# A masked-attention layer on one core: one sum behind the masks, first loads, bias and normalising moved, a decode and residual additions at the end by GpSimd

## The chip, the cores and the metric

The kernel runs on one core of a Trainium2 chip. The metric is device time in microseconds, as the median of several runs. The engines are TensorE (PE in the profile, with its weight loads as PEld), VectorE (DVE), ScalarE (ACT), GpSimd (POOL) and SyncE (SP), whose queue issues nearly all transfers. Each works through its own list in order; they wait for each other by semaphores.

## The reference

```python
# x, adj: (128, 128, 768) and (128, 128, 128); Wq, Wk, Wv: 768 x 768; H = 12 heads of HD = 64
h = jnp.maximum(_layernorm(x, axis=-1), 0.0)
q, k, v = (_split_heads(h @ W + b) for W, b in ((Wq, bq), (Wk, bk), (Wv, bv)))
scores = jnp.einsum('bhqd,bhkd->bhqk', q, k) / jnp.sqrt(HD)
scores = scores + beta * adj[:, None]
scores = jnp.where(adj[:, None] > 0, scores, -9000000000000000.0)
probs = jax.nn.softmax(scores, axis=-1)
out = jnp.einsum('bhqk,bhkd->bhqd', probs, v)
return x + out.transpose(0, 2, 1, 3).reshape(x.shape)
```

All of it is float32.

## The kernel before

**Groups and slices.** The 128 graphs are worked through in 32 groups of four (`GRP`, index `G`). Each group has three slices: `qk0` makes the queries and keys of heads 0 to 5, `v` the values of all heads, `qk1` the queries and keys of heads 6 to 11. The attention of a group is woven into the slices that follow its products.

**Products.** A slice is a product of the group's normalised activations with weights. The first group does it plainly (`plain_slice`, L845), and DVE and POOL meanwhile make sums of weight blocks, which are written to DRAM (`kept`). From the second group on (`product_z`, L550) each slice is 15 products with fewer multiplications than the plain way: product `n` of the list `PRODUCTS` takes one sum of activation blocks (`S0`, `S7`, ... or a block itself, `A00`, ...) and one prepared sum of weights (`T7`, `B01`, ..., read back from DRAM through a ring of five buffers by `load_T`, L338, or resident). The four chains "a" to "d" accumulate in a PSUM pair each, out of four pairs; scores and attention take their pairs from the same four, in the order in which pairs are given back.

**Evacuation.** After each product its result is taken to the output chunks that it belongs to, named (r, j). The first product of a chunk copies it, on ACT (L568 and two L570 with the bias); each later one adds to it on DVE (L574). Product 10 (S0) adds to chunk (0, 2), product 6 (A00) subtracts from it, product 7 (S7) adds to (0, 0). When a chunk has its last product, it is decoded in four additions (`decode`, L592 to L595), on POOL or, for some products, on DVE.

**What stands where.** The order of products in a slice is a list: `PORDER` for `qk0` and `v`, `ZORDER` for the second group's `qk0`, `QORDER` for `qk1`, `LORDER` for the last group's `qk1`. All other work is hung by hand on the positions of these lists: `then(at, ...)` puts it between the product's matmuls and its evacuation, `then((at, "post"), ...)` behind the evacuation. In each position the order of emission is: matmuls, masks that are due, work hung there, decodes and additions that are due, evacuation, exponentials that are due, the work hung behind. Thus the order on each engine is fixed. The work around the change is

- `sum_acts` (L467, DVE): an activation sum; S7 = A01 - S10 and S0 = S1 - S6 of the group,
- `scores` (L629, PE) and behind it the mask (L637, DVE), which reads the scores' PSUM pair, adds the bias of the adjacency and gives the pair back; the exponential (L639) follows on ACT,
- `attend` (L686, PE), which takes a pair at the next product and is woven into its matmuls; L695, L697 and L669 on ACT sum, copy and divide, `add` (L711, DVE) adds the residual, `send` stores,
- `norm` (L449, ACT): the normalisation and relu of the next group, in eight pieces of 192 columns for two graphs; `to_hT` (L462, DVE) transposes them,
- `halve_bias` (L977, POOL): a difference of the value bias, needed by the first `product_z` slice `v`.

In `qk0` of the third and later groups, scores stand at position 2 (twice) and behind position 6; S7 is hung at position 0, S0 at position 1.

**The end.** The last group's `qk1` is followed by attention in halves: `scores_half` (L738), its mask (L743) and `attend_half` (L759 on PE, L656 and L657 on DVE, `o_last` L669 on ACT, the addition L789 on DVE).

Of the kernel before, what the change touches and what calls it, by code (L numbers as in the profile page):

```python
# [14 lines left out]
ALU = mybir.AluOpType  # L15
# [4 lines left out]
GRP = 4  # L20
# [91 lines left out]
PORDER = (1, 0, 5, 2, 3, 10, 7, 6, 13, 11, 4, 9, 14, 8, 12)  # L112
ORDER = {"qk0": PORDER, "v": PORDER, "qk1": QORDER}
RING = 5
# [12 lines left out]
def direct(ctx, tc, x, adj, wq, bq, wk, bk, wv, bv, beta, out, bad):  # L127
# [10 lines left out]
    nc = tc.nc  # L138
    B, N, D = x.shape
    HD = D // HEADS  # L140
# [128 lines left out]
    def prepare(sl):  # L269
# [47 lines left out]
        for first, then_finish in PREPARED:  # L317
            for name in first:
                steps.append(lambda name=name: sums(name))
            for name in then_finish:  # L320
                steps.append(lambda name=name: finish(name))
# [123 lines left out]
    def norm(G, g, lo=0, hi=NB):  # L445
        for b in range(lo, hi):
            t = xg[G, g][:, b, :]
            n = g * NB + b
            nc.scalar.activation(t, t, AF.Relu, bias=shift[G, n], scale=rstd[G, n])  # L449

    def home_A(G, name):
        if (G, name) in wide:
            return A[G, name]
        t = wide[G, name] = work.tile([P, 2 * GRP, P], F32, tag=name, name=f"{name}_{G}", bufs=1 + (name[1] == "0"))
        full[G, name] = t[:, 0:7]
        A[G, name] = t[:, GRP:2 * GRP].rearrange("p (c g) n -> p c (g n)", c=2)
        return A[G, name]
# [76 lines left out]
    def product_z(G, sl, n):  # L534
# [21 lines left out]
        for (r, j), sign in uses:  # L556
# [19 lines left out]
            if not left[key]:  # L576
                last = order_of(G, sl) is LORDER
                engine = nc.vector if sl == "qk1" and (n == 12 or last and n in (11, 13, 14)) else nc.gpsimd
                later(lambda r=r, j=j, engine=engine: decode(G, sl, r, j, engine), 1 if last else LAG.get((sl, n), 1))
# [96 lines left out]
    def attend_steps(G, oc, behind):  # L676
# [14 lines left out]
        o = e.rearrange("p i w -> p (i w)")[:, 0:8 * VE].rearrange("p (r b e) -> p r b e", r=2, e=VE)  # L691
        t = xo[G, oc]

        def leave_pair():
# [15 lines left out]
        def add():  # L710
            nc.vector.tensor_tensor(t, t.rearrange("p g (i d) -> p g i d", i=2),  # L711
                                    o[:, :, :, 0:HD].rearrange("p r (g i) d -> p (r g) i d", i=2), ALU.add)

        def send():
            nc.sync.dma_start(out[G * GRP:(G + 1) * GRP, :, oc * P:(oc + 1) * P].rearrange("g n d -> n g d"), t)

        ends = G == NG - 1
        later(add, behind)
# [28 lines left out]
    def attend_half(G, oc, r, late, now=True):  # L747
# [30 lines left out]
        def sum_up():  # L778
# [9 lines left out]
            else:  # L788
                nc.vector.tensor_add(t, t, o.rearrange("p (b j) d -> p b (j d)", j=2))  # L789
            send()  # L790
# [160 lines left out]
    def half(step):  # L951

        if step == 0:
            for g in range(2, GRP):
                stats(0, g)
        elif step == 1:
            first["got"] = moments_1(0, 2 * NB, 4 * NB)
        else:
            first["pool"] = moments_2(0, 2 * NB, 4 * NB, *first["got"])
            for g in range(2, GRP):  # L960
                norm(0, g)
            for k in range(3):
                first["dve"] = to_hT(0, 1, k)
# [20 lines left out]
    def then(at, f, *args):  # L984
        todo.setdefault(at, []).append(lambda: f(*args))
# [72 lines left out]
    for n in range(18):  # L1058
        then(n, step, 2 - (n > 8))
    then(1, halve_bias)  # L1060
    sums_at(1, ((12, "S1"), (13, "S9"), (14, "S10"), (15, "S2")))
# [4 lines left out]
    bias(1, 4, 6, 8)  # L1066
    for n in range(RING):
        then(10 + n, load_T)
    plain_slice(0, "qk1", todo, (1, 0))

    for G in range(1, NG):
# [5 lines left out]
        attention(G - 1, 1, ((7, 2), (10, 0), (12, 1)))  # L1077
        sums_at(G, ((0, "S7"), (1, "S0"), (5, "S5"), (8, "S14"), (9, "S11")))
        if G == 1:
            todo[0].insert(0, lambda: sum_acts(1, "S6"))  # L1080
        if more:
            for n, at in enumerate((1, 2, 4, 5)):
# [198 lines left out]
```

## Time and profile before

| | us |
|---|---|
| median of 3 runs | 2697.48 |
| the runs | 2691.35, 2700.34, 2697.48 |
| the profiled execution | 2692.31 |
| its span, first to last instruction | 2690.5 |
| PE busy | 2650.9 |
| DVE busy | 2185.2 |
| POOL busy | 2111.8 |
| ACT busy | 1751.2 |

The profile is of one execution. A matmul's end is modelled, so that a busy PE is not yet a PE at its peak; a wait shows where an engine had nothing to do until another released it. Line numbers are those of the kernel before.

### The profile page before, as it was taken

Reading aid. Unit: us, or ns where it says so; the run is one execution under the profiler, and the core shown is the slowest. Engines: PE = TensorE matmul, PEld = TensorE weight load, DVE = VectorE, ACT = ScalarE, POOL = GpSimd, SP = SyncE. Lnnn points to the kernel's source line nnn. Section 1 sums busy time; section 2 is a strip of 40 time slices with the busy share of each in tenths; the row PEclk is TensorE's granted clock in tenths of the full one; section 3 lists DMA queues with packets and bytes.
Section 4 is the critical chain, followed back from the end, with each engine's and each line's share of the span. In section 5 each row is a group of like instructions: output and inputs, shape, how many; then the busy total and the mean of one; then the engine's idle time right before and its main releaser. Section 6 shows DMA issues by size and latency. Waiting matters only on the chain.

```text
span 2690.5 us, 121410 instructions
## 1 busy us (share of the span) xinstructions
PE 2650.9 (99%) x52029; PEld 2564.3 (95%) x52029; DVE 2185.2 (81%) x2705; ACT 1751.2 (65%) x4612; POOL 2111.8 (78%) x3034
## 2 busy tenths in 40 slices
PE   8999999999999999999999999999999999999997
PEld 7799999999999999999999999999999999999997
DVE  6878888878888788888788877788887888887886
ACT  2576766677666677666766666776667676667553
POOL 4867878877888778788778787787887787887783
PEclk9999999999999999999999999999999999999999
DMA  9889888989889898889898888888898988898875
GB/s 228 275 258 280 276 273 271 275 277 272 270 268 286 262 285 274 272 275 281 264 279 279 264 272 271 271 279 271 278 273 267 278 283 270 272 284 268 257 238 155
DMA packets 530341, 721.71 MB, mean 268 GB/s; under 512 B 105980, under 2 KB 374024, under 8 KB 529800
## 3 DMA queue, kind: packets, MB, share of 16 engines
q1 hardware_dynamic: 528640, 713.12, 85.9%
q8 instruction: 411, 6.73, 1.0%
q10 hardware_dynamic: 1160, 0.79, 0.2%
q14 instruction: 130, 1.06, 0.1%
HBM read 647.73 MB, written 66.05 MB: 265 GB/s over the span
## 4 chain that ended last, share of the span: by engine, by line
PE 77%; DVE 13%; DMA 3%; issue 2%; POOL 1%; ACT 0%; SPq 0%; POOLq 0%; DVEq 0%; ACTq 0%
PE pair L550 67%; PE pair L686 5%; PE pair L629 5%; DVE home L574 4%; DVE sbig L467 3%; DVE e L637 1%; DMA T_qk<-kept_qk 1%; DMA T_v<-kept_v 1%; DMA out_dram<-xo 1%; DVE xo L711 1%; DVE home L595 1%; DVE home L593 1%; DVE home L592 1%; DVE sbig L574 0%; DVE home L594 0%
## 5 line engine op out<-in xcount | busy, mean ns | idle before, releaser
L574 DVE TENSOR_TENSOR home<-home,pair 128x896 f32<-128x896 f32 x810 | 860.9, 1076 | 276.0 <-PE pair L550 236.9
L550 PE MATMUL pair<-sbig,T_qk 128*64 128x128 f32 x13020 | 827.8, 273 | 9.7 <-DVE e L637 7.3
L550 PEld LDWEIGHTS pair<-sbig,T_qk 128*64 128x64 f32 x13020 | 708.0, 137 | 20.9 <-DVE e L637 14.0
L550 PE MATMUL pair<-A,T_qk 128*64 128x128 f32 x6944 | 463.7, 273 | 0.0
L669 ACT ACTIVATE e<-e,sm 128x64 f32<-128x64 f32 x1512 | 382.0, 343 | 111.7 <-DVE sm L657 111.5
L592 POOL TENSOR_TENSOR home<-home 128x256 f32<-128x256 f32 x297 | 265.8, 895 | 226.2 <-DVE home L574 222.2
L550 PE MATMUL pair<-T_v,sbig 128*64 128x128 f32 x6944 | 418.3, 274 | 5.5 <-issue 2.8
L686 PE MATMUL pair<-v,e 128*64 128x65 f32 x6048 | 401.8, 221 | 0.5 <-DVE e L637 0.5
L550 PEld LDWEIGHTS pair<-T_v,sbig 128*64 128x64 f32 x6944 | 381.5, 137 | 20.1 <-issue 17.4
L568 ACT ACTIVATE home<-pair 128x640 f32<-128x640 f32 x325 | 231.2, 711 | 260.3 <-PE pair L550 200.0
L550 PEld LDWEIGHTS pair<-A,T_qk 128*64 128x64 f32 x6944 | 378.1, 137 | 5.9 <-issue 5.5
L686 PEld LDWEIGHTS pair<-v,e 128*64 128x64 f32 x6048 | 359.8, 137 | 3.9 <-DVE e L637 1.0
L550 PE MATMUL pair<-sbig,res_qk 128*64 128x128 f32 x4340 | 288.5, 273 | 0.0
L593 POOL TENSOR_TENSOR home<-home 128x256 f32<-128x256 f32 x297 | 248.4, 836 | 23.3
L595 POOL TENSOR_TENSOR home<-home 128x256 f32<-128x256 f32 x297 | 240.3, 809 | 23.3
L550 PEld LDWEIGHTS pair<-sbig,res_qk 128*64 128x64 f32 x4340 | 234.6, 137 | 5.3 <-issue 5.3
L695 ACT ACTIVATE sm<-pair,tiny 128x8 f32<-128x8 f32 x189 | 49.3, 261 | 286.9 <-PE pair L686 286.9
L594 POOL TENSOR_TENSOR home<-home 128x128 f32<-128x128 f32 x297 | 213.9, 720 | 23.3
L449 ACT ACTIVATE x<-x,block 128x192 f32<-128x192 f32 x480 | 231.8, 553 | 0.0
L637 DVE SCALAR_TENSOR_TENSOR e<-pair,biasT 128x1024 f32<-128x1024 f32 x189 | 225.0, 1216 | 3.2 <-PE pair L629 3.2
L639 ACT ACTIVATE e<-e 128x1024 f32<-128x1024 f32 x189 | 193.7, 1065 | 47.0 <-DVE e L637 39.1
L472 POOL TENSOR_TENSOR A<-A 128x256 f32<-128x256 f32 x186 | 169.9, 914 | 59.2 <-DVE A L462 59.2
(197 smaller groups left out, 4604.3 us busy)
## 6 DMA issues: line engine op xcount, KB each, us to landing
T_qk<-kept_qk SPq DMA_DIRECT2D x713, 448.0 KB, 4.9
T_v<-kept_v SPq DMA_DIRECT2D x341, 448.0 KB, 4.7
xo<-in_x_dram SPq DMA_DIRECT2D x189, 256.0 KB, 4.4
out_dram<-xo SPq DMA_DIRECT2D x189, 256.0 KB, 6.0
x<-in_x_dram SPq DMA_DIRECT2D x248, 192.0 KB, 6.7
sbig<-in_x_dram SPq DMA_DIRECT2D x116, 384.0 KB, 6.3
kept_qk<-prep_qk SPq DMA_DIRECT2D x23, 448.0 KB, 2.9
adj<-in_adj_dram SPq DMA_DIRECT2D x128, 64.0 KB, 4.5
```

The source lines that it names most:

```text
L449: nc.scalar.activation(t, t, AF.Relu, bias=shift[G, n], scale=rstd[G, n])
L550: nc.tensor.matmul(p[q:q + HD, at, :], lhs[:, q:q + HD], rhs, start=(first and at % 4 == 0), stop=True, skip_group_check=True)
L568: nc.scalar.activation(t[:, 0:5], p[:, 0:5], AF.Copy, scale=float(sign))
L574: nc.vector.tensor_tensor(t, t, p[:, 0:7], op)
L592: e.tensor_tensor(t[:, 1:4:2], t[:, 1:4:2], twice(5), ALU.add)
L593: e.tensor_tensor(t[:, 2:5:2], t[:, 2:5:2], twice(1), ALU.add)
L594: e.tensor_tensor(t[:, 4], t[:, 4], t[:, 6], ALU.add)
L595: e.tensor_tensor(t[:, 0:7:6], t[:, 0:7:6], twice(2), ALU.add)
L637: nc.vector.scalar_tensor_tensor(e, ps, SCORE_CAP * ISCALE, bias, op0=ALU.min, op1=ALU.add)
L639: trailing.append(lambda: nc.scalar.activation(e, e, AF.Exp, scale=1.0 / ISCALE))
L669: nc.scalar.activation(o[:, r, b, 0:HD], pa[:, r, b, 0:HD], AF.Copy, scale=t[:, 1, r, b:b + 1])
L686: nc.tensor.matmul(pa[q:q + HD, 2 * g + i, :], k[:, q:q + HD], vt[G, "v", r, h // 4][:, 4 * g + h % 4, :], start=True, stop=True, skip_gro ...
```

## The change

- Third to last group, `qk0`: products 7 and 6 change places (`XORDER`); S0 is hung at position 0 and S7 behind position 4. In the second group the sums move likewise, its order stays.
- First group: of the third and fourth graph's normalisation DVE does the third's (four scale-and-shift pieces and one maximum), ACT the fourth's. The first two loads of prepared weights are issued between two steps of the preparation instead of at positions 10 and 11 of the first `qk1`. The steps behind them come up to two places later. The bias step moves to position 4 of the second group's `qk0`.
- Last group: the decode behind product 13 and the residual additions of three chunks and of two halves go from DVE to POOL.

```diff
 PORDER = (1, 0, 5, 2, 3, 10, 7, 6, 13, 11, 4, 9, 14, 8, 12)
-ORDER = {"qk0": PORDER, "v": PORDER, "qk1": QORDER}
+XORDER = (1, 0, 5, 2, 3, 10, 6, 7, 13, 11, 4, 9, 14, 8, 12)
+ORDER = {"qk0": XORDER, "v": PORDER, "qk1": QORDER}
...
             for name in first:
                 steps.append(lambda name=name: sums(name))
+            if sl == "qk1" and first[0] == "T0":
+                steps += [load_T, load_T]
...
+    def norm_dve(G, g):
+        for b in range(NB):
+            t = xg[G, g][:, b, :]
+            n = g * NB + b
+            nc.vector.tensor_scalar(t, t, rstd[G, n], shift[G, n], op0=ALU.mult, op1=ALU.add)
+        t = xg[G, g]
+        nc.vector.tensor_scalar(t, t, 0.0, None, op0=ALU.max)
...
-                engine = nc.vector if sl == "qk1" and (n == 12 or last and n in (11, 13, 14)) else nc.gpsimd
+                engine = nc.vector if sl == "qk1" and (n == 12 or last and n in (11, 14)) else nc.gpsimd
...
         def add():
-            nc.vector.tensor_tensor(t, t.rearrange("p g (i d) -> p g i d", i=2),
-                                    o[:, :, :, 0:HD].rearrange("p r (g i) d -> p (r g) i d", i=2), ALU.add)
+            e = nc.gpsimd if ends and oc < 3 else nc.vector
+            t2 = t.rearrange("p g (i d) -> p g i d", i=2)
+            e.tensor_tensor(t2, t2, o[:, :, :, 0:HD].rearrange("p r (g i) d -> p (r g) i d", i=2), ALU.add)
...
-                nc.vector.tensor_add(t, t, o.rearrange("p (b j) d -> p b (j d)", j=2))
+                (nc.gpsimd if now else nc.vector).tensor_tensor(t, t, o.rearrange("p (b j) d -> p b (j d)", j=2), ALU.add)
...
-            for g in range(2, GRP):
-                norm(0, g)
+            norm_dve(0, 2)
+            norm(0, 3)
...
-    then(1, halve_bias)
...
-    for n in range(RING):
+    for n in range(2, RING):
         then(10 + n, load_T)
...
-        sums_at(G, ((0, "S7"), (1, "S0"), (5, "S5"), (8, "S14"), (9, "S11")))
+        sums_at(G, ((0, "S0"), ((4, "post"), "S7"), (5, "S5"), (8, "S14"), (9, "S11")))
         if G == 1:
             todo[0].insert(0, lambda: sum_acts(1, "S6"))
+            then(4, halve_bias)
```

More of the change, by code (lines that the diff above doesn't have):

```diff
@@ L692, in attend_steps @@
         t = xo[G, oc]
+        ends = G == NG - 1
         def leave_pair():
@@ L710, in add @@
         def add():
-            nc.vector.tensor_tensor(t, t.rearrange("p g (i d) -> p g i d", i=2),
-                                    o[:, :, :, 0:HD].rearrange("p r (g i) d -> p (r g) i d", i=2), ALU.add)
+            e = nc.gpsimd if ends and oc < 3 else nc.vector
+            t2 = t.rearrange("p g (i d) -> p g i d", i=2)
+            e.tensor_tensor(t2, t2, o[:, :, :, 0:HD].rearrange("p r (g i) d -> p (r g) i d", i=2), ALU.add)
         def send():
             nc.sync.dma_start(out[G * GRP:(G + 1) * GRP, :, oc * P:(oc + 1) * P].rearrange("g n d -> n g d"), t)
-        ends = G == NG - 1
         later(add, behind)
```

## The prediction

> **What bounds the kernel now.** I read the busy times first, then the stretches, then who waited for whom, then one group on three engines.
>
> ```profile
> span 2690.5 us, 121410 instructions
> ...
> PE 2650.9 (99%) x52029; PEld 2564.3 (95%) x52029; DVE 2185.2 (81%) x2705; ACT 1751.2 (65%) x4612; POOL 2111.8 (78%) x3034
> ```
>
> ```profile
> 0.00:207.00 207.00, 196.49 (x2431) 168.84 (x2433) 157.67 (x288) 99.03 (x250) 139.50 (x232) 0.99 0.87 253
> ```
>
> ```profile
> 288.60:370.10 81.50, 81.20 (x1650) 79.45 (x1648) 67.37 (x80) 55.47 (x146) 66.05 (x95) 1.00 0.89 276
> ```
>
> ```profile
> 2591.00:2690.50 99.50, 85.03 (x1688) 79.94 (x1684) 66.40 (x116) 44.34 (x124) 42.98 (x66) 0.94 0.59 180
> ```
>
> In the last three rows the first number after the stretch is its length, the second the time in which TensorE (PE) was busy. PE is busy for 2650.9 of 2690.5 us, so all that a rearrangement can win is the remaining 39.6 us. Of these, 10.5 us lie in the first 207 us (the first two groups), 14.5 us in the last 99.5 us, and in the middle a group of 81.5 us has 0.3 us of idle PE. The change removes no matmul; it can only move these waits. Which of them it can move, the waits of the weight loads say best, since they run ahead of the matmuls and show the whole gap:
>
> ```profile
> PEld pair L550 <- DVE e L637: 14.7, 29, 0.7
> ```
>
> So 29 times PE waits for a mask (L637), 14.7 us in all, 0.51 us each: once in each group from the fourth on. This is what "a sum behind the masks" aims at. Here is the place in one group, PE first, then VectorE (DVE), ScalarE (ACT) and GpSimd (POOL); columns are start, duration, engine, line, what is written from what, count, and the idle time before with its releaser.
>
> ```profile
> 298.09 1.98 PE L629 MATMUL pair<-home 64*64 64x128 f32 x64
> ...
> 302.05 4.81 PE L550 MATMUL pair<-sbig,T_qk 128*64 128x128 f32 x84 [0.30 <-DVE e L637]
> 306.79 1.10 PE L629 MATMUL pair<-home 64*64 64x128 f32 x32
> 307.82 1.75 PE L550 MATMUL pair<-A,T_qk 128*64 128x128 f32 x28
> ...
> 309.62 0.40 PE L686 MATMUL pair<-v,e 128*64 128x65 f32 x8
> ```
>
> ```profile
> 298.17 1.42 DVE L467 TENSOR_TENSOR sbig<-A,sbig 128x896 f32<-128x896 f32 x1
> 299.52 1.34 DVE L467 TENSOR_TENSOR sbig<-sbig 128x896 f32<-128x896 f32 x1
> 300.79 2.34 DVE L637 SCALAR_TENSOR_TENSOR e<-pair,biasT 128x1024 f32<-128x1024 f32 x2
> ...
> 303.95 1.07 DVE L574 TENSOR_TENSOR sbig<-sbig,pair 128x896 f32<-128x896 f32 x1
> 304.95 1.08 DVE L467 TENSOR_TENSOR sbig<-A,sbig 128x896 f32<-128x896 f32 x1
> 307.00 1.09 DVE L574 TENSOR_TENSOR home<-home,pair 128x896 f32<-128x896 f32 x1 [0.97 <-PE pair L550]
> 308.01 1.22 DVE L637 SCALAR_TENSOR_TENSOR e<-pair,biasT 128x1024 f32<-128x1024 f32 x1
> ```
>
> ```profile
> 302.06 0.72 ACT L568 ACTIVATE home<-pair 128x640 f32<-128x640 f32 x1
> ...
> 303.15 2.04 ACT L639 ACTIVATE e<-e 128x1024 f32<-128x1024 f32 x2
> 305.04 1.02 ACT L449 ACTIVATE x<-x,block 128x192 f32<-128x192 f32 x2
> 305.92 0.74 ACT L568 ACTIVATE home<-pair 128x640 f32<-128x640 f32 x1
> 306.50 0.67 ACT L570 ACTIVATE home<-pair,bqk 128x128 f32<-128x128 f32 x2
> ```
>
> The two sums S7 (298.17) and S0 (299.52) stand ahead of the two masks on DVE. The first mask ends at 300.79 + 2.34/2 = 301.96, and the product at position 4 (the x84 row, three products), which takes the PSUM pair that this mask gives back, starts at 302.05.
>
> **Steady groups: the wait goes, and another one takes most of its place.** With S7 gone from there, S0 starts at 298.2 and the first mask about 1.3 us earlier, well before the pair is wanted. PE starts positions 4 to 6 0.51 us sooner. S7 itself (1.08 by the row at 304.95, which has no other work beside it) fits between the evacuation at 303.95 and the next sum: both sums are done by about 306.5, and product 7, now at position 7, wants S7 only at 307.3. So far the gain is the whole 0.51 us.
>
> But the new order also puts product 6 (A00) at position 6, right behind product 10 (S0) at position 5. Both write the same chunk, (0, 2): product 10 comes first, so ACT evacuates it (305.92 and 306.50, two L570 ending at 307.17), and product 6 is then added to it by DVE. In the old order product 7 stood between, whose evacuation adds to another chunk and waited for PE alone (the row at 307.00). The new evacuation must wait for ACT. ACT is not moved by the change: from the row at 302.06 on it works without a gap, on things queued before the masks matter. So the evacuation begins at about 307.21, 0.21 later than now, and the third mask, queued behind it on DVE, ends at 308.01 + 1.22 + 0.21 = 309.44 instead of 309.23. The attention at 309.62 takes the pair that this mask gives back. PE, 0.51 us early, would want it at 309.11; it gets it at about 309.49 (a mask's end to PE took 0.09 in the x84 row, less with the pair of masks rounded: I take 0.05). What remains of 0.51 is 0.13 us. For the 28 groups before the last of these that is 3.6 us; the last group has no normalisation of a following one on ACT (L449), so there the whole 0.5 us stays. The third group does not wait for a mask now, and may get the new wait: 0.3 us back. Sum: 3.8 us. Ends: 0 (ACT 0.13 us later than I think) and 14.7 us (ACT not in the way). S0 a slot earlier, and (0, 2) decoded a slot earlier by POOL, cost nothing: POOL sits idle before that decode,
>
> ```profile
> 310.86 1.51 POOL L592 TENSOR_TENSOR home<-home 128x256 f32<-128x256 f32 x1 [6.23 <-DVE home L574]
> ```
>
> for 6.23 us. If that cover were gone, the chunk is needed only in the next slice.
>
> **First group and the way into the second.**
>
> ```profile
> 28.43 3.61 ACT L449 ACTIVATE x<-x,shift,rstd 128x192 f32<-128x192 f32 x8 [3.12 <-POOL shift L397]
> ```
>
> ```profile
> 32.08 1.90 DVE L462 STREAM_TRANSPOSE A<-x 128x512 f32<-128x512 f32 x3 [5.71 <-ACT x L449]
> ...
> 112.30 0.68 DVE L493 TENSOR_SCALAR adj<-biasT 128x512 f32<-128x512 f32 x1
> ```
>
> ```profile
> 32.84 15.81 PE L845 MATMUL pair<-A,sbig 128*128 128x256 f32 x72 [1.53 <-DVE A L462]
> ...
> 115.75 0.45 PE L686 MATMUL pair<-v,e 128*64 128x65 f32 x8 [0.51 <-DVE e L637]
> ...
> 126.93 1.75 PE L550 MATMUL pair<-sbig,T_qk 128*64 128x128 f32 x28 [0.89 <-DMA T_qk<-kept_qk]
> 128.89 4.80 PE L550 MATMUL pair<-sbig,T_qk 128*64 128x128 f32 x84 [0.20 <-DMA T_qk<-kept_qk]
> ...
> 136.24 1.70 PE L550 MATMUL pair<-sbig,T_qk 128*64 128x128 f32 x28
> ```
>
> ACT's eight normalisations take 3.61 us; half of them 1.8. DVE, idle for 5.71 us, does the other half beside it: by the 0.68 us for 512 columns, four of 192 columns about 0.25 each and one maximum over 768 about 1.0, together 2.0 us or less. The transposes start 1.6 us earlier, and PE's 1.53 us go. The two early loads of weights go out where SP's queue stands still for the prepared sums; they wait only for buffers whose writes are queued ahead of them, and take away 0.89 + 0.20 us. What stands behind them on SP, a residual load and later prepared writes, waits for GpSimd or is needed much later. Without the bias step (below) GpSimd, and through its prepared sums DVE, run about 1.4 us ahead there, so that the 0.51 us at 115.75 go too. That makes 3.1 us.
>
> ```profile
> 96.45 1.45 POOL L977 TENSOR_TENSOR bv_b<-bv_b 128x384 f32<-128x384 f32 x1
> ```
>
> The bias step lands in the second group at position 4, where POOL is idle; its first user is the V slice. But in the second group product 7 stays at position 5 (its order is not changed), and S7 is now queued after position 4, behind a mask:
>
> ```profile
> 135.79 1.21 DVE L637 SCALAR_TENSOR_TENSOR e<-pair,biasT 128x1024 f32<-128x1024 f32 x1
> ```
>
> The mask can start only when the scores before position 4 are done; mask and sum, 1.2 + 1.05, run against one product of 1.6 us (three took 4.74 us from 302.05 to 306.79). So PE waits there at least 0.7 us, and about 1.5 if DVE is a microsecond behind as it is now. Sum for this part: 3.1 - 1.5 = 1.6 us gained, between -0.5 and 2.8.
>
> **The end.**
>
> ```profile
> 2661.60 0.72 POOL L595 TENSOR_TENSOR home<-home 128x256 f32<-128x256 f32 x1
> ```
>
> ```profile
> 2662.20 0.67 PE L738 MATMUL pair<-home 64*64 64x128 f32 x16
> ```
>
> ```profile
> 2663.93 0.42 DVE L592 TENSOR_TENSOR home<-home 128x256 f32<-128x256 f32 x1
> ...
> 2665.16 0.42 DVE L595 TENSOR_TENSOR home<-home 128x256 f32<-128x256 f32 x1
> ...
> 2668.53 0.43 DVE L789 TENSOR_TENSOR xo<-xo,o_last 128x256 f32<-128x256 f32 x1 [1.06 <-ACT o_last L669]
> ...
> 2673.47 0.42 DVE L789 TENSOR_TENSOR xo<-xo,o_last 128x256 f32<-128x256 f32 x1 [1.05 <-ACT o_last L669]
> ```
>
> From 2662 on DVE sets the pace. It loses a decode (2663.93 to 2665.58, 1.6 us), an addition behind it, and the two halves' additions with the waits for ACT before them, 1.49 and 1.47 us. Not all of it is on the path: with the decode gone DVE waits for PE's product instead, and of the two waits the second counts. On the other side GpSimd now does a 128x512 addition (about 1.4 us, twice the 0.72 for 256 columns) ahead of the decode that ends at 2662.3 and that the scores at 2662.20 wait for: PE and all after it get 1.3 us later there. Followed through, the third half's scores come 0.25 us earlier, the fourth's 0.75, the last two 2.1 us earlier, and the tail with them. I take 2.0 us, between 0 and 2.5.
>
> A rule of the Trainium skill speaks against this part: "SBUF — State Buffer", section "Who interferes with whom", says that a DVE instruction with two SBUF inputs and a GpSimd instruction that reads SBUF exclude each other, the second waiting until the first has ended. The trace agrees so far: the same 128x256 operation of GpSimd took 1.51 us at 310.86, beside DVE's sums, and 0.72 at 2661.60. By that rule each GpSimd addition at the end could hold up a DVE decode for its whole length; only one, of 256 columns, meets a decode in the order that I followed, so by the rule the end would gain 1.3 and the sum be 6.7 instead of 7.4.
>
> **Sum.** 3.8 + 1.6 + 2.0 = 7.4 us. The profiled execution took 2692.31 us, 5.2 less than the median 2697.48 of the three runs; it becomes 2684.9, and the median 2690.1. A measurement of this kernel tells about 0.3%, 8.1 us, from no change, so the likeliest case stands just on that border.
>
> **Rivals.** (a) The masks' wait goes and nothing follows: if ACT's evacuation of product 10 ends before PE has done product 6, the groups keep 14.7 us. For it speaks that 0.4 us less on ACT would do; against it that ACT has no gap there. 14.7 + 1.6 + 2.0 = 18.3 us, median 2679.2. (b) Slower: the evacuation that now waits for ACT ends later still. The point from which it decides is 0.13 us beyond the 307.21 at which I let it begin. ACT has a pair of normalisations of 1.02 us right ahead (305.04); if one more piece of 0.6 us comes between on ACT, each group is 0.47 us longer than now, 28 groups 13.2 us, less the 3.6 at both ends: 9.6 us slower, 2707.1 at the median. Against it: no ACT instruction in the groups is added or moved. (c) The part in the groups does nothing at all and start and end cancel (POOL's delay before the scores, S7 in the second group): 2697.
>
> **How the numbers follow.** My case 0.58, (a) 0.2, (b) 0.12, (c) 0.1. My case spreads by some 3 us, so about half of it, 0.3, is beyond 0.3% faster, and a little of it, 0.01, slower. With (a) this makes 0.5 for faster. (b) gives 0.1 to slower; with 0.03 for what I have not seen, 0.14. The rest is 0.36. The range goes from 2677, just past (a), to 2698, past (c); it leaves out (b) and what lies beyond (a).
>
> **What would show it.** Right: in the waits, the 14.7 us of L550 for the mask shrink below 2, and a new entry of about 0.4 us, some 28 times, appears for the attention's matmuls behind a mask; on DVE the evacuation at position 6 names ACT as its releaser; a group is 0.1 us shorter. At the start the 1.53 us of idle PE are gone; in the second group position 5 waits for a sum; at the end the scores wait 1.1 us or more for a GpSimd decode and DVE's two additions with their waits for ACT (1.06 and 1.05) are gone. Wrong: groups 0.5 us shorter with no new wait (a), or longer (b).

## The result: 0.3% faster, as forecast, but not by the terms of its sum

| | us |
|---|---|
| before, median of 6 runs | 2695.86 (2691.35 to 2700.34) |
| after, median of 6 runs | 2685.23 (2683.14 to 2687.57) |
| after / before | 0.9968, 95% interval 0.9957 to 0.9978 |
| profiled execution before and after | 2692.31, 2685.37 |
| its span before and after | 2690.5, 2683.5 |

The forecast was 2690.1, between 2677 and 2698. The medians of the table differ by 10.6 us, but before's lies high in its six runs: in the 23 runs that it had beside four of the experiments its median was 2692.01, and 2685.23 is 6.8 us or 0.25% below that. The two profiled executions differ by 6.9 us where the sum said 7.4, so that the gain lies on the border of 0.3%, as forecast. That agreement is luck in part: of the three terms the one on which most of the argument was spent is nearly gone, and the other two are larger.

Most line numbers of after are 11 to 12 higher: L561 is the product (L550), L640 the scores (L629), L697 the attention (L686), L648 the mask (L637), L478 the sums (L467), L585 the adding evacuation (L574), L579 and L581 ScalarE's (L568, L570), L452 the normalisation (L449, only 3 higher), L458 and L460 VectorE's share of it (new), L750 the halves' scores (L738), L603 to L606 the decode, L725 and L801 the additions (L711, L789), L709 ScalarE's copy of an attention pair (L697). In the kernel without the early loads they are 2 lower than in after.

The page after the change, and the three stretches that were shown of before:

```profile
span 2683.5 us, 121478 instructions
...
PE 2654.5 (99%) x52029; PEld 2564.6 (96%) x52029; DVE 2179.1 (81%) x2701; ACT 1750.2 (65%) x4608; POOL 2073.5 (77%) x3043
```

```profile
0.00:207.00 207.00, 200.07 (x2495) 173.36 (x2497) 161.42 (x295) 99.61 (x254) 145.24 (x235) 0.98 0.88 260
288.60:370.10 81.50, 81.26 (x1648) 79.36 (x1646) 67.10 (x80) 55.44 (x147) 64.50 (x95) 1.00 0.87 271
2584.00:2683.50 99.50, 87.29 (x1766) 82.06 (x1762) 64.56 (x109) 47.14 (x133) 51.01 (x78) 0.96 0.63 187
```

TensorE is busy 3.6 us more in the first 207 us, 2.3 us more in the last 99.5, and in a middle group about as before. To share out the 7.0 us of the span, one event is followed: the double scores with which each `qk0` from the third group on has its first attention work. The first and the last of these rows, before and then after:

```profile
216.23 1.98 PE L629 MATMUL pair<-home 64*64 64x128 f32 x64
...
2588.73 1.98 PE L629 MATMUL pair<-home 64*64 64x128 f32 x64
```

```profile
212.85 1.98 PE L640 MATMUL pair<-home 64*64 64x128 f32 x64
...
2584.57 1.98 PE L640 MATMUL pair<-home 64*64 64x128 f32 x64
```

| part | before | after | gain | forecast |
|---|---|---|---|---|
| start, to the third group's double scores | 216.23 | 212.85 | 3.38 | 1.6 |
| 29 groups between | 2372.50 | 2371.72 | 0.78 | 3.3 |
| from there to the end | 101.77 | 98.93 | 2.84 | 2.5 |

(The forecast's 3.8 for the groups held 0.5 for the last one, which lies in the third part here.) So the change brought its gain at the two ends, and the edit behind the masks, meant for every group, next to nothing.

**In the groups** the weight loads' waits have changed names, as forecast. They no longer wait for the mask at the product but at the attention:

```profile
PEld pair L697 <- DVE e L648: 12.6, 29, 0.5
PEld pair L561 <- ACT e L709: 5.0, 28, 0.4
```

The first row is the wait foretold ("about 0.4 us, some 28 times": 12.6 / 29 = 0.43). The second was not foretold. One group, TensorE, then its weight loads, VectorE and ScalarE:

```profile
294.48 1.98 PE L640 MATMUL pair<-home 64*64 64x128 f32 x64
...
305.89 0.45 PE L697 MATMUL pair<-v,e 128*64 128x65 f32 x8 [0.24 <-DVE e L648]
```

```profile
309.80 1.51 PEld L561 LDWEIGHTS pair<-A,T_qk 128*64 128x64 f32 x28 [0.16 <-ACT e L709]
```

```profile
303.61 1.09 DVE L585 TENSOR_TENSOR home<-home,pair 128x896 f32<-128x896 f32 x1 [0.81 <-ACT home L581]
304.61 1.22 DVE L648 SCALAR_TENSOR_TENSOR e<-pair,biasT 128x1024 f32<-128x1024 f32 x1
```

```profile
302.90 0.67 ACT L581 ACTIVATE home<-pair,bqk 128x128 f32<-128x128 f32 x2
...
305.93 1.06 ACT L650 ACTIVATE e<-e 128x1024 f32<-128x1024 f32 x1 [1.48 <-DVE e L648]
...
309.17 0.58 ACT L709 COPY e<-pair 128x520 f32<-128x520 f32 x1
```

VectorE's evacuation now names ScalarE's as its releaser (303.61, L581), the third mask comes late behind it, the attention waits 0.24 us for that. Counted from the double scores, the attention starts at 305.89 - 294.48 = 11.41; before it was 309.62 - 298.09 = 11.53. The gain of 0.12 us is the 0.13 of the forecast. But the chain goes on: behind the late mask comes the exponential, then row statistics, then the copy that gives the attention's pair back, and a product takes this pair and waits for it (the weight load at 309.80). Counted from the double scores, the copy starts at 309.17 - 294.48 = 14.69, before the change at 312.56 - 298.09 = 14.47. That takes the 0.12 back and a little more.

**At the start** the 1.53 us before the plain matmuls and the waits for the first weights are gone; the wait for S7 in the second group is there, at its lower bound:

```profile
26.39 21.33 PE L857 MATMUL pair<-A,sbig 128*128 128x256 f32 x96
...
133.88 1.75 PE L561 MATMUL pair<-sbig,T_qk 128*64 128x128 f32 x28 [0.67 <-DVE sbig L478]
```

**At the end** GpSimd's addition stands ahead of a decode, whose result the scores wait for (2658.66), and the last scores still wait for VectorE:

```profile
2654.58 1.18 POOL L725 TENSOR_TENSOR xo<-xo,e 128x512 f32<-128x512 f32 x1
```

```profile
2658.66 0.45 PE L750 MATMUL pair<-home 64*64 64x128 f32 x8 [0.36 <-POOL home L606]
...
2672.36 1.16 PE L750 MATMUL pair<-home 64*64 64x128 f32 x16 [1.79 <-DVE home L605]
```

### The profile page after: what moved, and what is told of

It reads as the page before. It is cut to its first block, busy times and chain, and to the rows that moved or that the text cites. A ratio compares the mean times of both kernels' runs of the same rounds, so it can differ in the third digit from the quotient of the medians.

```text
span 2683.5 us, 121478 instructions
## 1 busy us (share of the span) xinstructions
PE 2654.5 (99%) x52029; PEld 2564.6 (96%) x52029; DVE 2179.1 (81%) x2701; ACT 1750.2 (65%) x4608; POOL 2073.5 (77%) x3043
## 3 DMA queue, kind: packets, MB, share of 16 engines
q8 instruction: 411, 6.73, 1.0%
## 4 chain that ended last, share of the span: by engine, by line
PE 48%; POOL 27%; ACT 12%; issue 5%; DMA 5%; DVE 3%; SPq 1%; ACTq 0%; POOLq 0%; DVEq 0%
PE pair L561 36%; PE pair L697 4%; POOL v L618 4%; PE pair L857 3%; PE pair L640 3%; POOL v L617 3%; POOL home L616 3%; POOL A L483 3%; ACT x L452 3%; ACT e L650 2%; POOL home L603 2%; POOL home L605 2%; ACT home L579 2%; ACT home L581 2%; POOL v L614 2%
## 5 line engine op out<-in xcount | busy, mean ns | idle before, releaser
L585 DVE TENSOR_TENSOR home<-home,pair 128x896 f32<-128x896 f32 x810 | 861.1, 1076 | 276.2 <-PE pair L561 223.8
L561 PE MATMUL pair<-sbig,T_qk 128*64 128x128 f32 x13020 | 832.8, 273 | 2.9 <-DMA T_qk<-kept_qk 2.0
L561 PEld LDWEIGHTS pair<-sbig,T_qk 128*64 128x64 f32 x13020 | 707.8, 137 | 12.7 <-issue 6.9
L561 PE MATMUL pair<-A,T_qk 128*64 128x128 f32 x6944 | 465.3, 273 | 0.4 <-ACT e L709 0.4
L603 POOL TENSOR_TENSOR home<-home 128x256 f32<-128x256 f32 x298 | 246.6, 828 | 267.8 <-DVE home L585 260.1
L561 PE MATMUL pair<-T_v,sbig 128*64 128x128 f32 x6944 | 417.4, 274 | 1.5 <-issue 1.5
L697 PE MATMUL pair<-v,e 128*64 128x65 f32 x6048 | 400.8, 221 | 5.6 <-DVE e L648 5.5
L579 ACT ACTIVATE home<-pair 128x640 f32<-128x640 f32 x325 | 231.7, 713 | 261.4 <-PE pair L561 200.9
L561 PEld LDWEIGHTS pair<-T_v,sbig 128*64 128x64 f32 x6944 | 381.5, 137 | 14.9 <-issue 13.1
L561 PEld LDWEIGHTS pair<-A,T_qk 128*64 128x64 f32 x6944 | 376.9, 137 | 5.4 <-ACT e L709 5.0
L697 PEld LDWEIGHTS pair<-v,e 128*64 128x64 f32 x6048 | 355.5, 137 | 15.6 <-DVE e L648 12.6
L561 PE MATMUL pair<-sbig,res_qk 128*64 128x128 f32 x4340 | 288.3, 273 | 0.0
L606 POOL TENSOR_TENSOR home<-home 128x256 f32<-128x256 f32 x298 | 239.7, 804 | 23.4
L604 POOL TENSOR_TENSOR home<-home 128x256 f32<-128x256 f32 x298 | 229.8, 771 | 23.4
L561 PEld LDWEIGHTS pair<-sbig,res_qk 128*64 128x64 f32 x4340 | 234.5, 137 | 5.3 <-issue 5.3
L452 ACT ACTIVATE x<-x,block 128x192 f32<-128x192 f32 x480 | 232.9, 557 | 0.0
L605 POOL TENSOR_TENSOR home<-home 128x128 f32<-128x128 f32 x298 | 212.6, 713 | 23.4
L648 DVE SCALAR_TENSOR_TENSOR e<-pair,biasT 128x1024 f32<-128x1024 f32 x189 | 225.1, 1217 | 4.7 <-PE pair L640 4.7
```

What stands on the lines that cost most here:

```text
L561: nc.tensor.matmul(p[q:q + HD, at, :], lhs[:, q:q + HD], rhs, start=(first and at % 4 == 0), stop=True, skip_group_check=True)
L579: nc.scalar.activation(t[:, 0:5], p[:, 0:5], AF.Copy, scale=float(sign))
L585: nc.vector.tensor_tensor(t, t, p[:, 0:7], op)
L603: e.tensor_tensor(t[:, 1:4:2], t[:, 1:4:2], twice(5), ALU.add)
L604: e.tensor_tensor(t[:, 2:5:2], t[:, 2:5:2], twice(1), ALU.add)
L605: e.tensor_tensor(t[:, 4], t[:, 4], t[:, 6], ALU.add)
```

## Experiments

All were compared with the kernel before on the same chips. Effects of less than about 5 us were read from the traces, by the three parts above. The five experiments on the start and the end ran once each, so that their whole times decide nothing. The start is counted there from the first group's small 128x16 products, since the time until these, 23.4 to 26.2 us, differs from run to run for every kernel: before 216.23 - 25.64 = 190.6, after 212.85 - 26.16 = 186.7. By this count the start gained 3.9 us. It still differs between runs of one program: in two kernels below that are changed in the last group alone (`e6_first_add_dve` and `e7_end_undone`) the start took 190.8 and 187.7 us, in the changed kernel 186.7. So what an edit does to the start is read from single waits.

### What holds the groups: ScalarE's evacuation

```diff
 # e1_norm_later
-            for n, at in enumerate((1, 2, 4, 5)):
+            for n, at in enumerate((1, 2, 5, 6)):
                 then((at, "post"), norm, G + 1, n // 2, n % 2 * 2, n % 2 * 2 + 2)   # qk0
 # e2_s0_first
-XORDER = (1, 0, 5, 2, 3, 10, 6, 7, 13, 11, 4, 9, 14, 8, 12)
+XORDER = (1, 0, 5, 2, 10, 3, 6, 7, 13, 11, 4, 9, 14, 8, 12)
```

The first moves two pieces of normalisation on ScalarE from ahead of the evacuation of product 10 to behind it; the second leaves ScalarE alone and gives product 10 a slot more. Expected of the first:

> The changed kernel, with ACT's last two pairs of normalisations in the slice qk0 one place later (behind positions 5 and 6 instead of 4 and 5), so that they no longer stand ahead of the evacuation of product 10. Theory A (the wait for the mask was replaced by a wait of DVE for that evacuation, and this alone holds the third mask and with it the attention and, over ACT, the next pair): the evacuation ends 1.0 us earlier, DVE's evacuation at position 6 is released by PE, the attention starts 11.0 us after the double scores instead of 11.4, an undisturbed group takes 80.95 us instead of 81.53, and the whole is 14 to 17 us faster than the changed kernel, about 2670. Rival B (the groups are held by the transfers, busy for 88% of the time): the 11.4 shrink to 11.0, but the time comes back as waits for T_qk and T_v; 0 to 4 us faster than the changed kernel.

and of the second:

> The changed kernel with product 10 ahead of product 3 in qk0 (positions 4 and 5 exchanged), normalisations as in the changed kernel. Product 10 and product 6 are then two positions apart and ACT evacuates product 10 ahead of the normalisations behind position 4. Theory A: as when the normalisations are put later, a group of about 80.95 us and 14 to 17 us less than the changed kernel. If only the order of ACT's work mattered in some other way (its copies, not the addition to chunk (0, 2)), the third mask would stay where it is, at 11.4. Rival B: 0 to 4 us faster.

Measured: 2673.75 us (ratio 0.9924, 0.9908 to 0.9940) and 2674.01 us (0.9929, 0.9912 to 0.9947); both spans are 2672.4. The group of the first, one row each of ScalarE, VectorE and TensorE:

```profile
301.00 0.68 ACT L581 ACTIVATE home<-pair,bqk 128x128 f32<-128x128 f32 x2
```

```profile
301.81 1.09 DVE L585 TENSOR_TENSOR home<-home,pair 128x896 f32<-128x896 f32 x1
```

```profile
293.47 1.98 PE L640 MATMUL pair<-home 64*64 64x128 f32 x64
...
304.47 0.40 PE L697 MATMUL pair<-v,e 128*64 128x65 f32 x8
```

ScalarE's evacuation ends at 301.68, before VectorE wants it, the adding evacuation names no releaser any more, and the attention starts at 11.00 without a wait. An undisturbed group takes 80.95 us, against 81.53 after and 81.46 before. Two edits that have only this in common, the time of ScalarE's evacuation against VectorE's, do the same, so this evacuation is shown to be what took the masks' 0.5 us back.

The size was a miss: 0.58 us in each of 29 groups would be 17 us, and the span fell by 11.1. The mean group, by the double scores, is 81.44 us, 0.49 over the undisturbed one; after the change this excess was 81.78 - 81.53 = 0.25. It lies in waits like this one of the first experiment, for which the profile names no releaser:

```profile
732.13 0.44 PE L640 MATMUL pair<-home 64*64 64x128 f32 x4 [1.92 <-issue]
```

### What the irregular waits are

```diff
 # e10_half_loads, on e1_norm_later
     def load_T():
         if nt[0] < len(ring):
             G, sl, n = ring[nt[0]]
             nt[0] += 1
+            if G > 2 and nt[0] % 2:
+                tz[G, sl, n] = nt[1]
+                return
-            t = tz[G, sl, n] = work.tile(...)
+            t = nt[1] = tz[G, sl, n] = work.tile(...)
```

> The kernel with the normalisations later, which from the fourth group on leaves out every second load of streamed weights: the product uses the tile of the product before it, so part of the products is computed with other weights, at the same cost on TensorE. It asks what the irregular waits of TensorE are, those that the profile puts to issue, and which took back a part of what later normalisations gain. My account: the page lists 411 packets, 6.73 MB, of instructions that go over the same 16 DMA engines as the data, which are busy for 0.89 of the time in the groups; the waits are for late instructions. With some 225 of 722 MB gone the engines are at 0.6 to 0.65, these waits (7.9 us between the third and the last group) fall below 2, the mean group goes from 81.44 to 80.95 to 81.15, the span from 2672.4 to 2660 to 2665. Rival, that instructions are late for another reason (their own order, a place in the program): the waits stay at 6 to 10 us, the span at 2669 to 2676.

The program has a second branch, a plain and slow path that it takes behind the last group where a sum of the softmax is out of bounds. The mixed-up weights led into it, so that the whole took 20089 us, and the forecast for the span can't be compared. The groups had run before that, at their own speed, and the other two parts of the forecast can. The same 2250 us of them, first of the kernel with later normalisations and all loads, then with half the loads; the columns behind the clock are the transfer engines' busy share and GB/s:

```profile
300.00:2550.00 2250.00, 2241.16 (x45416) 2195.96 (x45414) 1858.28 (x2182) 1526.77 (x4012) 1756.86 (x2597) 1.00 0.89 275
```

```profile
300.00:2550.00 2250.00, 2249.75 (x45680) 2207.75 (x45678) 1868.52 (x2194) 1532.21 (x4033) 1769.92 (x2614) 1.00 0.59 180
```

TensorE's idle time goes from 8.84 to 0.25 us, and the mean group is (2560.18 - 212.00) / 29 = 80.97. Both are as forecast. So the irregular waits come from full transfer engines, in a kernel that seems bound by TensorE alone. That these waits are for late instructions this does not show: no row names them, and with half the loads gone the weights themselves have more time too. The transfers in the traces say more. The page of after has an own line for those of instructions, "q8 instruction: 411, 6.73, 1.0%". Between 100 and 2570 us all fourteen runs together have 87 waits of TensorE over 0.3 us without a releaser, and 83 of them end 1.15 to 1.65 us after an instruction transfer of q8 has ended. One such transfer comes every 6.3 us, so by chance some 7 of the 87 would. The waits are therefore for instructions, as far as timing can show it. Why these come late is open: the transfers themselves took no less time with half the loads (1.07 us on average, 1.03 with all).

### The groups' edit alone, and all but it

```diff
 # e3_groups_only, on the kernel before: XORDER for qk0, and
+        sums_at(G, ((0, "S0"), ((4, "post"), "S7"), ...) if G > 1 else ((0, "S7"), (1, "S0"), ...))
 # e4_without_groups, on the changed kernel: PORDER for qk0, and
+        sums_at(G, ((0, "S7"), (1, "S0"), (5, "S5"), (8, "S14"), (9, "S11")))
```

> The kernel before with the group part alone: products 7 and 6 exchanged and S0 at position 0, S7 behind position 4, from the third group on; second group, start and end as before. Theory A: an undisturbed group takes 81.5 us, as before within 0.1, so the whole is within 3 us of the kernel before. If the group part is worth what the wait of 14.7 us said: 14 us faster.

> The changed kernel without the group part: order of products and sums of qk0 as before, in the second group too; start and end as changed. Theory A: all of the gain is in the two ends, so it is within 2 us of the changed kernel, 6 to 9 us faster than before; in the second group the wait of 0.67 us for a sum goes, groups take 81.45. If the groups carry the gain: as the kernel before.

Measured: 2689.88 us (0.9993, 0.9982 to 1.0004) and 2686.91 us (0.9978, 0.9966 to 0.9990). The edit behind the masks alone can't be told from no change; its undisturbed group is 81.53 with the attention at 11.40, as in the changed kernel. Without it the rest of the change keeps the gain; the group is 81.46 and the attention at 11.52, as before the change.

### The start

```diff
 # e5_second_group_undone: for G == 1 again
+        sums_at(G, ... if G > 1 else ((0, "S7"), (1, "S0"), ...))
 # e8_loads_late: the two early loads back to positions 10 and 11
-            if sl == "qk1" and first[0] == "T0":
-                steps += [load_T, load_T]
-    for n in range(2, RING):
+    for n in range(RING):
 # e9_norm_act
-            norm_dve(0, 2)
+            norm(0, 2)
```

> The changed kernel, in the second group alone S7 is summed ahead of S0 behind no mask again (positions 0 and 1). My account: the 0.67 us that TensorE waits at position 5 of the second group (133.88, for the sum S7) goes and no other wait comes in its place, since the second group's mask and sum then run beside other products; the third group's double scores (212.85 in the changed kernel) start up to 0.7 us earlier, 212.2 or so, if no irregular transfer wait falls in between. The third and later groups stay at 81.53. Rival, that S7's early sum costs as much at a mask in the second group (0.5 us, as in the groups of the kernel before): a wait of a product for a mask appears at position 4 of the second group, and 212.85 moves by 0.2 us or less.

> The changed kernel without the two early loads of weights (all five at positions 10 to 14 of the first group's last slice, as before). My account, that the loads were what the second group's first products waited for: TensorE waits again for T_qk in the second group, 0.89 and 0.20 us or a little less at 124 to 129, and the third group's double scores start 0.7 to 1.2 us later than 212.85. Rival, that the transfers' time varies from run to run and their place in the queue matters little: waits for T_qk there below 0.3 us and the same start within 0.4 us.

> The changed kernel with all of the first group's eight normalisations on ScalarE again. My account, that the 1.53 us wait for the transposes at the start is theirs: TensorE waits 1.5 us before the plain matmuls at about 32, and since VectorE and GpSimd set when the second group's S7 is there, part of it is given back as a shorter wait at position 5 of the second group (0.67 to 1.6 in the changed kernel): from the start's 128x16 products to the third group's double scores 187.2 to 188.5, against 186.7 in the changed kernel. Rival, that the start is set by the prepared sums alone and the split buys nothing: the same 186.7.

With S7 early in the second group again (span 2682.7, start 185.5) its wait of 0.67 us is replaced by one of 0.49 us for a mask:

```profile
136.69 1.10 PE L640 MATMUL pair<-home 64*64 64x128 f32 x32 [0.49 <-DVE e L648]
```

Only 0.2 us lies between these two; the other microsecond by which this start is shorter is an irregular wait of 1.38 us in the changed kernel's run (0.28 here). So the rival is right that S7's early sum costs a wait for a mask, though it comes at the scores two places on and not at position 4. Against this one run of the changed kernel the two places of S7 are worth the same; against the runs in which S7's late place costs 1.58 and 1.59 us (the two kernels changed in the last group alone) the early place would save 1.1 us. That stays open.

Without the early loads (span 2687.2, start 190.6) the double scores of the third group start at 213.93, 1.1 us later than in the changed kernel, as expected; but this run was 2.8 us ahead at the small products, so that by the count from these it is 3.9 us. The size of the wait was a clear miss. The first products of the second group:

```profile
125.69 7.68 PE L559 MATMUL pair<-sbig,T_qk 128*64 128x128 f32 x112 [3.06 <-DVE sm L666]
```

```profile
125.60:129.00 3.40, 3.31 (x36) 3.34 (x38) 3.27 (x5) 0.18 (x1) 3.24 (x4) 0.58 1.02 413
```

In the changed kernel the same products were:

```profile
124.22 6.29 PE L561 MATMUL pair<-sbig,T_qk 128*64 128x128 f32 x112
```

Here they wait 3.06 us. The profile names a reciprocal of VectorE that these products do not read; the first loads of `T_qk` go out 10 us later than in the changed kernel (118.07 against 107.83), and the first of them lands at 125.56, right before the products start, so the wait is for them. And then the 112 products take 7.68 us instead of 6.29: in the 3.4 us behind the wait the granted clock is 0.58 (in the row of the stretch, the number before 1.02; from 125.1 to 128.5 it is 0.50). In the kernel before the visible price was 0.89 + 0.20 us only, because TensorE came there later. How late it comes is in part a matter of the run: with the groups' edit alone, whose start is that of the kernel before, the wait for the same load was 2.41 us:

```profile
127.10 3.17 PE L551 MATMUL pair<-sbig,T_qk 128*64 128x128 f32 x50 [2.41 <-DMA T_qk<-kept_qk]
```

Wherever the loads go out late, these products start when the first of them has landed: 101.3 (kernel before), 102.1 (groups' edit alone) and 102.3 us (without the early loads) behind the small products, against 98.1 in the changed kernel. So behind late loads the other edits of the start bring this point no gain.

With the normalisations back on ScalarE (span 2683.1, start 211.08 - 23.47 = 187.6) the wait is there to the hundredth, and a wait of 0.96 us for S7 as well:

```profile
30.67 15.81 PE L857 MATMUL pair<-A,sbig 128*128 128x256 f32 x72 [1.53 <-DVE A L473]
...
132.94 1.75 PE L561 MATMUL pair<-sbig,T_qk 128*64 128x128 f32 x28 [0.96 <-DVE sbig L478]
```

The 187.6 is as expected, but one of the runs with the split had 187.7, so the total shows nothing. The two waits here are 2.49 us together, where the three runs with the split have 0.67 to 1.59 for S7 and, irregular waits aside, no other: the split is worth 0.9 to 1.8 us.

### The end

```diff
 # e6_first_add_dve
-            e = nc.gpsimd if ends and oc < 3 else nc.vector
+            e = nc.gpsimd if ends and oc in (1, 2) else nc.vector
 # e7_end_undone: the decode behind product 13 and all residual additions on VectorE again
```

> The changed kernel, but of the last group's three 128x512 additions by GpSimd the first (2654.58, 1.18 us, ahead of the decode that the scores at 2658.66 wait for) goes back to VectorE. My account, that GpSimd's addition delays that decode: the waits of the scores for GpSimd's decode (0.36 us of idle TensorE, 1.6 us in the weight loads) shrink to 0.4 us or less in the weight loads, the last stretch from the double scores of the last group to the end is 0.3 to 1.0 us shorter than 98.93. Rival, that VectorE sets the pace from there: its 0.7 us more come back at the decodes that it does, the last stretch is 98.9 to 99.6.

> The changed kernel without its three edits in the last group's end (the decode of chunk 13 and all residual additions back on the engines of the kernel before). My account, that the end is worth about 2.4 us by itself (2.84 less the 0.45 or so that the groups' edit gives the last group at its masks): from the last group's double scores to the end 101.3 (98.93 with the three edits, 101.77 before). Rival, that the end is shorter because the groups' edit brings the last group's work forward, and GpSimd's share gives nothing: 99 to 100.

With one addition less on GpSimd the stretch from the last double scores to the end is 2685.7 - 2587.48 = 98.2 us, 0.7 shorter than in the changed kernel's run (98.6 to 98.9 in the six runs with this end and the groups' edit); the scores' wait for a GpSimd decode is gone from TensorE's list, and what stays of it in the weight loads, "PEld pair L750 <- POOL home L606: 1.1, 1, 1.1", stood in the kernel before as well. (The whole span, 2685.7, is longer than after's for waits and 3.4 us of halved clock in its second group and for waits in its groups, which this edit does not touch.) With the end undone the stretch is 2684.7 - 2583.47 = 101.2, as expected to 0.1: the three edits of the end are worth 2.3 us, and 0.5 us of the 2.84 is the groups' edit in the last group, whose ScalarE has no next group to normalise. The pair of runs above shares it out a little otherwise: the stretch is 101.5 with the groups' edit alone and 99.2 with all but it, so that the end's own edits have 2.6 us and the groups' edit 0.2 to 0.3.

The trace of this last run also shows, at the second group's position 5,

```profile
132.85 1.75 PE L561 MATMUL pair<-sbig,T_qk 128*64 128x128 f32 x28 [1.58 <-DVE sbig L478]
```

the wait for S7 near the 1.5 us that the forecast gave it, where the changed kernel's own run has 0.67. Up to there the programs are the same. In this run TensorE was at its small products 2.6 us earlier (23.52 against 26.16), but VectorE had S7 only 1 us earlier: TensorE's lead becomes a wait for the sum.

### Two versions meant to be best

```diff
 # b1_best_norm: e1_norm_later, e6_first_add_dve and
-ZORDER = (1, 0, 3, 5, 2, 7, 10, 6, 11, 13, 4, 9, 14, 8, 12)
+ZORDER = (1, 0, 3, 5, 2, 10, 7, 6, 11, 13, 4, 9, 14, 8, 12)
 # b3_best_both: the same and the XORDER of e2_s0_first
```

> A version meant to beat both: the changed kernel with (1) the normalisations of the following group later (positions 1, 2, 5, 6 for 1, 2, 4, 5), (2) in the second group product 10 at position 5 and product 7 at 6, so that S7 has a slot more, (3) the first of GpSimd's three 128x512 additions back on VectorE. My account: (1) is worth about 11 us against the changed kernel as measured alone (2673.75), (2) takes the 0.67 to 1.6 us wait for S7, (3) 0.7 us; span 2670.5, time 2672, range 2668 to 2675, groups of 80.95. Rival, that what is taken away comes back in the irregular waits as part of (1) did: no better than 2673.7.

> As the other best version, and product 10 before product 3 in the groups as well (both remedies for ScalarE's late evacuation together). My account: one remedy already takes the whole wait, so the undisturbed group stays at 80.95 and the time within 2 us of the other best version's. Rival, that the evacuation's margin with one remedy is so small that single groups still wait, and two make the mean group shorter: 3 to 6 us faster than with one.

Measured: 2676.6 us (0.9946, 0.9932 to 0.9960) and 2678.61 us (0.9948, 0.9934 to 0.9962), no better than later normalisations alone. The undisturbed group is 80.95 in both, so that one remedy is enough, and two add nothing. What was meant for the second group made it worse:

```profile
133.17 1.75 PE L561 MATMUL pair<-sbig,T_qk 128*64 128x128 f32 x28 [2.31 <-ACT home L581]
```

The wait for S7 is gone, and TensorE waits 2.31 us (1.76 in the other) for an evacuation of ScalarE that stands behind eight divisions and a pair of normalisations. By the order of the evacuations it is that of product 5, which belongs to chain "a" as product 10 does: product 10, taken earlier, finds its PSUM pair not yet copied. As in the groups, an evacuation on ScalarE decides. The best version measured is the change with later normalisations, 2673.75 us, which beats both kernels; the exchange of products 10 and 3 (2674.01) is as good.

## Why the prediction was right, and where it was not

**Right: the mechanism in the groups, up to the attention.** The wait for the mask at position 4 is gone, the evacuation at position 6 waits for ScalarE, the attention waits 0.43 us in the weight loads, and starts 0.12 us earlier (0.13 forecast). In the last group, where 0.5 us were to stay, it starts 11.00 us behind the double scores instead of 11.32, 0.3 earlier. Rival (a), that nothing follows, fails because ScalarE's evacuation was late, as argued; the two experiments show that with this evacuation in time the groups are 0.5 us shorter than before, as (a) had it. Rival (b) fails: the evacuation was not later than assumed. Rival (c) was nearest to the truth for the groups, though not because nothing happened there.

**Mis-sized: "What remains of 0.51 is 0.13 us. For the 28 groups before the last of these that is 3.6 us."** The sum ended at the attention. ScalarE's exponential, statistics and copy behind the late third mask are late by the same 0.2 us, and a product takes the pair that this copy gives back. This step is shown by the rows (the copy 0.22 us later) and by the two experiments, in which it goes together with the late evacuation. An undisturbed group is thus 0.07 us longer than before, not 0.13 shorter: 29 times, 2 us lost. That the 29 groups are 0.78 us shorter all the same is 2.8 us less of irregular waits in the one execution than in the other, and these are not shown to be due to the change.

**Mis-sized: the start, 1.6 forecast and 3.4 measured.** The 3.1 us of waits that should go are gone. That the 0.51 us at 115.75 went through the change is not shown: with the groups' edit alone, and the start of the kernel before, it is gone too. Followed matmul by matmul from the small products, the changed kernel is 3.7 us ahead when the second group's first weights are there, more than 3.1, since TensorE's idle time shows only a part of each wait. It then loses 0.8 us at S7, where "about 1.5" was deducted, and gains 1.0 us behind that, half of it at a wait for a load at 214.55, which the sum did not have. The wait for S7 was 0.67 in this execution, and 0.67 to 1.59 in the others, so its bounds were right and its value varies from run to run. The loads' price was taken from the trace of before, 1.09 us, where TensorE was late; with the other edits in place the wait was 3.06 us, and the products behind it took 1.39 us more. The normalisation's 1.53 us were worth 0.9 to 1.8, according to the wait for S7. Edits in one chain are not worth the sum of the waits that they had before.

**Right: the end, 2.0 forecast and 2.3 to 2.6 measured.** The scores wait for GpSimd's decode behind an addition, though only 0.36 us where 1.1 or more was named as the sign; a cost of 0.7 us was forecast as 1.3, since the addition took 1.18 us instead of 1.4 and only a part of it reached the scores.

**The rule on shared SBUF access,** by which this part would have gained 1.3 us ("SBUF — State Buffer", "Who interferes with whom" in the Trainium skill): the end's own 2.3 to 2.6 us are nearer to the sum without it. It does bear, at one decode that runs beside GpSimd's addition at 2667.81:

```profile
2668.20 0.62 DVE L603 TENSOR_TENSOR sbig<-sbig 128x256 f32<-128x256 f32 x1
```

It takes 0.62 us instead of the 0.42 that the same operation takes elsewhere, so it lost 0.2 us. When it started, the addition (0.73 us) had 0.34 us left, and it ended 0.28 us behind the addition. One row can't tell whether it waited for the addition's end or was only slowed.

## What to carry to other kernels

Follow a delay until it meets slack, and not only to the next wait on the busiest engine: here 0.2 us on VectorE went over ScalarE to a PSUM pair and back to TensorE, four operations past the place where the sum stopped. When two neighbours in an order are exchanged, ask which engine evacuates the one that now comes first, and what stands ahead of that on its queue; moving two small pieces there was worth 11 us, the exchange itself nothing. And take the price of a wait in the schedule that the other edits leave, not in the one that shows it: the same late load cost TensorE 0.89, 2.41 and 3.06 us, by when TensorE came to it.

## What was not expected of the hardware

- A long wait of TensorE can be paid twice. Behind 3.06 us of waiting the granted clock was 0.58 for 3.4 us, and the same 112 products took 1.39 us more. Behind one of 1.74 us (the kernel with one addition less on GpSimd) it was 0.60 for 4 us, yet behind one of 1.92 us (later normalisations) 1.00. The low stretch itself is 3.4 us at 0.50 each time (125.1 to 128.5 in the one, 162.8 to 166.2 in the other). Of the eleven waits over 1.5 us between 100 and 2600 us in all runs, three are followed by one (1.74, 1.93 and 3.06 us), and those of 2.31 and 2.41 us are not. So the length of the wait alone does not decide it. "TensorE: Matmul & The Clock Gate", Part 1, of the Trainium skill says that the clock is halved after an idle window of about 3.4 us that runs freely; the drop to half and its length agree, and that waits of half that length have it in one run and not in another is not explained by a whole idle window.
- Full transfer engines cost TensorE time that no row explains, by the timing through late instructions: it was idle for 8.8 us in 2250 at a busy share of 0.89, 0.25 us at 0.59, and nearly all its waits without a releaser end 1.15 to 1.65 us behind an instruction transfer.
- VectorE's maximum over 128x768 took 0.64 us, less than the estimated 1.0:

```profile
30.40 0.64 DVE L460 TENSOR_SCALAR x<-x 128x768 f32<-128x768 f32 x1
```
